# A four-layer graph network on one core: layer 0 begins with x in chunks, and layers 2 and 3 become one run of steps

## The chip, the core and the metric

The kernel runs on one core of a Trainium2 chip. The core has five instruction streams that run side by side and wait for each other by semaphores: PE (TensorE: matrix products, into PSUM), DVE (VectorE), ACT (ScalarE: exp, tanh, square root, copies), POOL (GpSimd) and SP (SyncE, which here only issues DMAs). DMAs issued by SP go through one queue and those issued by POOL through another; both are carried by the core's 16 DMA engines. The metric is device time in microseconds (us); lower is better. PE has a granted clock, which the profile shows as a share of full speed.

## The reference

The input is x, 2708 nodes by 512 features, and adj, a dense 0/1 matrix of 2708 x 2708 with 1.2% ones and a full diagonal. Four layers follow each other, each as x = layernorm(x + layer(x)):

- **Layer 0**, four heads of 128 features. Per head: Xw = X W, f1 = Xw v1, f2 = Xw v2, and an attention softmax over the neighbours of sigmoid(f1[i] + f2[j]). It is applied to Xw, then batch norm, a dense block with elu, batch norm, the same attention again on the result, the product with W transposed, elu, and a second dense block.
- **Layer 1**: adj times (x W + b), divided by the column sums of adj.
- **Layer 2**: h = x edge_w; scores h h^T, masked by adj, softmax along a row; adj times a softmax over nodes times that, applied to x weight.
- **Layer 3**: full attention: query, key and value projections, scores scaled, plus adj twice, softmax, applied to the values.

The first part of layer 0 and layers 2 and 3, as the reference has them:

```python
Xw = jnp.einsum('hnd,hde->hne', Xh, W)
f1 = jnp.einsum('hnd,hd->hn', Xw, V[:, 0, :, 0])
f2 = jnp.einsum('hnd,hd->hn', Xw, V[:, 1, :, 0])
sig = jax.nn.sigmoid(f1[:, :, None] + f2[:, None, :])
...
h = x @ edge_w
e = jnp.where(adj > 0, h @ h.T, NEG_BIG)
edge_att = jax.nn.softmax(e, axis=1)
output = adj * (node_att * edge_att) @ (x @ weight) + bias
...
a = (x @ Wq + bq) @ (x @ Wk + bk).T * scale + adj_matrix + spatial_matrix
attn = jax.nn.softmax(a, axis=-1) @ (x @ Wv + bv)
```

## The kernel before

All of it is float32. The nodes are cut into NT = 22 blocks, 21 of 128 and a last one of 20.

**Who sets the order.** The kernel is written in program order, but a planner in the language lays the instructions out: from its own estimate of times it puts on each engine the instruction that comes first in program order among those that are ready, and it gives out tile buffers ("bufs" of a tag in a pool) as they come free. On the chip each engine then works through its list in that order and waits where it has to. So an instruction can move ahead of others when its inputs and a buffer are free, and SP's list of DMA issues is in that order too.

**Start of layer 0** (`project`, L199). SP loads the parameters (L77), w0T (L190), w0, v1, v2 (L205 to L208) and then xT in four loads, each of 128 feature rows by all 2708 nodes (L210). PE makes w v1 and w v2 (L213). f1 is needed in two shapes. For the first pair of heads and the first half of the nodes it is made directly on all 128 partitions (`f1b`): matmuls with w v1 repeated 128 times as the stationary operand (L223), copied out by DVE and ACT (L227). For the rest it is made as rows (L231: 32 columns per head, six chunks of nodes), copied (L239), stored in DRAM as f1_d by POOL (L240), and loaded back by SP, spread over the partitions (L363). Then the values: for each of the 22 blocks, four heads of X W together with f2 go to a PSUM tile pxw (L245), which ACT or DVE copies to xw (L253), and DVE takes f2h out (L257). pxw lives under the PSUM tags po0 to po2.

**Attention of layer 0** (`attention_pass`, L285, called with first=True for the first attention, and again for the second). The loops run over two halves of the destination nodes (hf), two pairs of heads (p), and the 22 source blocks (jt). One step of it (`form`, L309): SP loads a block `a` of adjT, 128 x 1354 (L315, four buffers); in the first pair of each half DVE turns it into a mask (L330, L331) and POOL stores that as adj_d (L335); ACT takes tanh of f1b plus f2h for two heads (L341); DVE adds a constant and multiplies by the mask (L349); ACT takes exp (L350). PE then multiplies with the values: 2 heads x 3 column chunks into six accumulators `po`, tags po0 to po2 again (L397), and sums with ones (L420). The tiles po are allocated ahead of the loops (L354). The broadcast f1b of each later pair has two buffers and is loaded at L363 as early as a buffer allows.

**Layers 2 and 3** (`softmax_layer`, L1024, called once for each). The 22 blocks of destination nodes form 7 groups: six of three blocks, and the last of four (blocks 18 to 21). For each group there are 22 score steps and 22 sum steps, one per source block. A score step (`one_score`) loads a block of adjT columns (a_cols), makes scores by PE (L1106, `ps_s`), masks or biases them on DVE (L1397 or L1454) and keeps a running maximum (L1154). In layer 2 the scores are symmetric, so blocks already computed are stored, loaded again as s_kept, and transposed (L1098). At the end of a group `spread_max` brings the maximum of each row to all partitions, by transposes (L1166) and a product with ones (L1177). A sum step (`one_sum`) subtracts the maximum on DVE (L1197), takes exp on ACT (L1198), adds to the row sums (L1208), in layer 2 multiplies by adj (L1400), and PE multiplies with the values into `po` (L1213). The values are `sup` in layer 2 and the x rows themselves, `xs`, in layer 3, where the projection by wv comes after (`project`, L1288). At a group's end `end` takes reciprocals and queues the rest in `later`: in layer 2 the residual (L1406), the layer norm, and the transposes into hT, the keys and queries of layer 3 (L1412).

The steps of all groups are one sequence of 154. The sum step of number t - 25 is traced with the score step of number t:

```python
lag = NT + AHEAD
for t in range(steps + lag):
    if t < steps:
        ... one_score(states[gi], k)
    if t >= lag:
        ... one_sum(states[gi], k)
```

So the last 25 steps of a layer have sums and no scores. The two layers open their buffers (`att`, `att_ps`) each for itself; layer 3 begins when layer 2 has ended and its buffers and `sup` are given back. It then loads mqk (the product of wq and wk transposed, L1435), wv (L87) and bv (L92), and projects its first query (L1015).

Of the kernel before, what the change touches and what calls it, by code (L numbers as in the profile page):

```python
# [17 lines left out]
P = 128  # L18
# [11 lines left out]
def gnn_stack_kernel(  # L30
# [46 lines left out]
    nc.sync.dma_start(prm_sb, prm)  # L77
# [78 lines left out]
    with ExitStack() as l0:  # L156
# [31 lines left out]
        nc.vector.tensor_scalar(bm1, prm_sb[:, MB_DEC, :], 1.0, None, ALU.subtract)  # L188
        w0T_sb = p0.tile([P, H, P], F32, name="w0T_sb")
        nc.sync.dma_start(w0T_sb, w0T)  # L190
# [8 lines left out]
        def project(att, psum):  # L199
# [5 lines left out]
            nc.sync.dma_start(w0x[:, :, :P], w0)  # L205
            v12 = att.tile([P, H, 2], F32, tag="v12", name="v12", bufs=1)
            nc.sync.dma_start(v12[:, :, 0], v1)
            nc.sync.dma_start(v12[:, :, 1], v2.rearrange("(h e) -> e h", h=H))  # L208
            for c in range(C):
                nc.sync.dma_start(xT_sb[:, c, :], xT[c * P : (c + 1) * P, :])  # L210
# [6 lines left out]
            wv1 = held[:, H * (P + 2) : H * (2 * P + 2)].rearrange("p (h e) -> p h e", h=H)  # L217
            nc.vector.tensor_copy(wv1, w0x[:, :, P : P + 1].to_broadcast([P, H, P]))
            f1b = att.tile([P, HP, HW], F32, tag="f1b", name="f1b")
            for k in range(HP):  # L220
                for q, (q0, w) in enumerate(HCH[0]):
                    pf = psum.tile([P, HP, BANK], F32, tag=f"po{q}", name="pf")[:, k, :]
                    nc.tensor.matmul(  # L223
                        pf[:, :w], wv1[:, k, :], xT_sb[:, k, q0 : q0 + w], start=True, stop=True
                    )
                    copy = nc.scalar.copy if q % 2 else nc.vector.tensor_copy
                    copy(f1b[:, k, q0 : q0 + w], pf[:, :w])  # L227
            for ci, (c0, w) in enumerate(CHUNKS):
                pf = psum.tile([P, BANK], F32, tag=f"psm{ci % 2}", name="pf")
                for h in range(H):  # L230
                    nc.tensor.matmul(  # L231
                        pf[32 * h : 32 * h + 32, :w],
                        wv1[:, h, :32],
                        xT_sb[:, h, c0 : c0 + w],
                        start=True,
                        stop=True,
                    )
                f1c = att.tile([P, BW], F32, tag="rs", name="f1c")
                nc.vector.tensor_copy(f1c[:, :w], pf[:, :w])  # L239
                nc.gpsimd.dma_start(f1_d[:, c0 : c0 + w], f1c[0 : 32 * H : 32, :w])  # L240
            for jt, (j0, n) in enumerate(BLOCKS):
# [10 lines left out]
                copy = nc.vector.tensor_copy if jt % 3 == 2 else nc.scalar.copy  # L252
# [11 lines left out]
            copies(xw[:, NT - 1, :])  # L264
            copies(f2h[:, NT - 1, :])
            return f1b
# [18 lines left out]
        def attention_pass(values, first, att, psum, finish, f1b=None):  # L285
# [23 lines left out]
            def form(hf, p, jt, att, prepare, f1b, tv):  # L309
# [3 lines left out]
                a = att.tile([P, HW], F32, tag="a", name="a", bufs=4 if first else 3)  # L313
                src = adjT if prepare else adj_d
                nc.sync.dma_start(a[:n, :w], src[j0 : j0 + n, h0 : h0 + w])  # L315
# [33 lines left out]
                nc.vector.scalar_tensor_tensor(tv, tv, GUARD, ab, ALU.add, ALU.mult)  # L349
                nc.scalar.activation(tv, tv, AF.Exp, scale=0.5)  # L350

            later = []

            both = [  # L354
                psum.tile([P, HP, BANK], F32, tag=f"po{q}", name="po", bufs=1) for q in range(HB)
            ]
            po = [both[q][:, k, :] for k in range(HP) for q in range(HB)]
            for hf, (h0, w) in enumerate(HSPAN):
                for p in range(H // HP):
                    prepare = first and p == 0  # L360
                    if f1b is None or not prepare or hf > 0:
                        f1b = att.tile([P, HP, HW], F32, tag="f1b", name="f1b", bufs=2)
                        nc.sync.dma_start(  # L363
                            f1b[:, :, :w],
# [1173 lines left out]
```

## Time and profile before

| what | us |
|---|---|
| median of 3 runs | 3347.64 (3344.58 to 3348.74) |
| the profiled execution | 3344.3 |
| its span, first to last instruction | 3342.5 |
| PE busy | 3251.5 |
| first attention product of layer 0 begins | 52.71 |
| layer 2 begins (first score) | 1686.16 |
| layer 3 begins (first score) | 2389.58 |

A line of the profile's timeline gives start and length in us, engine, line of the kernel, operation, output<-inputs, shape, and how many such instructions it merges; in brackets the idle time of the engine just before it and what ended it. A line of the waits gives engine, tile and line of who waited, "<-" whom it waited for, then total us, how many times, and the longest. A line of the stretches gives the window, its length, the busy us of PE, PE's weight loads, DVE, ACT and POOL with counts, then PE's granted clock, the busy share of the DMA engines and GB/s. PE's ends are modelled, so a busy PE is not always at its peak.

### The profile page before, as it was taken

How to read it: one execution, taken by the hardware profiler on the slowest of the kernel's cores; microseconds unless marked ns; L12 is line 12 of the kernel's file. 1: busy time of each engine (PE TensorE's matmuls, PEld its weight loads, DVE VectorE, ACT ScalarE, POOL GpSimd, SP SyncE). 2: the span in 40 equal slices, each digit the busy share in tenths (PEclk: the TensorE clock that was granted, in tenths of full speed). 3: DMA queues.
4: the chain of work that ended last, by engine and by line, in shares of the span. 5: the costliest groups of instructions: out<-in, count | busy, mean ns of one | idle time of the engine just before them, and what ended most of it. 6: DMA issues, size and time to landing. Idle time of an engine off the chain costs nothing.

```text
span 3342.5 us, 30573 instructions
## 1 busy us (share of the span) xinstructions
PE 3251.5 (97%) x10980; PEld 1741.6 (52%) x10980; DVE 1988.9 (60%) x3227; ACT 1347.6 (40%) x1518; POOL 130.7 (4%) x212
## 2 busy tenths in 40 slices
PE   8999999999999989999999999999999999999998
PEld 5444444544444445885555555444455555555554
DVE  7868978767687585445135677776253443443533
ACT  6888887468877652001133333332011010110110
POOL 1100100000000000000010000000000000000001
PEclk9999999999999999999999999999999999999999
DMA  7655753335535412540044444553211111111100
GB/s 284 248 172 187 275 195 102 121 106 185 187 126 166 152 40 76 144 129 15 0 129 127 122 129 131 148 146 95 70 44 36 42 33 42 40 34 45 33 23 20
DMA packets 168576, 367.58 MB, mean 110 GB/s; under 512 B 20870, under 2 KB 111710, under 8 KB 165032
## 3 DMA queue, kind: packets, MB, share of 16 engines
q1 hardware_dynamic: 153448, 301.77, 30.2%
q0 software_dynamic: 14976, 63.86, 5.1%
q8 instruction: 86, 1.41, 0.2%
q14 instruction: 66, 0.54, 0.0%
HBM read 301.67 MB, written 63.35 MB: 109 GB/s over the span
## 4 chain that ended last, share of the span: by engine, by line
PE 72%; issue 13%; DVE 9%; DMA 3%; ACT 3%; POOL 1%; SPq 0%; POOLq 0%; DVEq 0%; ACTq 0%
PE po L1213 21%; PE ps_s L1106 17%; PE po L397 9%; PE ps_nb L954 6%; PE ps_wide L1015 4%; DVE t L349 3%; PE ps_hid L118 2%; PE ps_sup L1356 2%; PE ps_o L1291 2%; PE ps_mlp L637 1%; DMA a<-adj_d 1%; PE ps_dec L733 1%; ACT t L341 1%; DMA a_cols<-in_adjT_dram 1%; ACT t L350 1%
## 5 line engine op out<-in xcount | busy, mean ns | idle before, releaser
L349 DVE SCALAR_TENSOR_TENSOR t<-t,a 128x2708 f32<-128x2708 f32 (+1 forms) x162 | 480.0, 2975 | 142.4 <-ACT t L341 140.4
L341 ACT ACTIVATE t<-f1b,f2h 128x1354 f32<-128x1354 f32 (+1 forms) x324 | 445.8, 1414 | 87.9 <-PE psm L420 42.7
L350 ACT ACTIVATE t<-t 128x2708 f32<-128x2708 f32 (+1 forms) x162 | 396.7, 2452 | 71.1 <-DVE t L349 69.7
L397 PE MATMUL po<-t,xw 128*128 128x452 f32 (+3 forms) x1056 | 416.2, 557 | 8.1 <-ACT t L350 4.0
L397 PE MATMUL po<-t,emb 128*128 128x452 f32 (+3 forms) x1056 | 404.4, 552 | 16.7 <-ACT t L350 9.0
L1213 PE MATMUL po<-sup,e 128*128 128x512 f32 x882 | 410.3, 602 | 5.5 <-DVE e L1400 5.3
L1213 PE MATMUL po<-e,xs 128*128 128x384 f32 (+1 forms) x1176 | 407.5, 489 | 0.0
L1106 PE MATMUL ps_s<-q,hT 128*128 128x384 f32 (+1 forms) x1176 | 403.5, 489 | 0.0
L1454 DVE SCALAR_TENSOR_TENSOR e<-a_cols,ps_s 128x384 f32<-128x384 f32 (+1 forms) x154 | 85.6, 556 | 419.3 <-PE ps_s L1106 396.2
L397 PEld LDWEIGHTS po<-t,emb 128*128 128x128 f32 (+1 forms) x1056 | 195.6, 192 | 218.9 <-issue 195.0
L1106 PEld LDWEIGHTS ps_s<-q,hT 128*128 128x128 f32 x1176 | 222.6, 190 | 161.5 <-issue 6.5
L397 PEld LDWEIGHTS po<-t,xw 128*128 128x128 f32 (+1 forms) x1056 | 190.8, 192 | 220.6 <-issue 201.8
L1213 PEld LDWEIGHTS po<-e,xs 128*128 128x128 f32 x1176 | 221.6, 190 | 157.2 <-issue 6.0
L1213 PEld LDWEIGHTS po<-sup,e 128*128 128x128 f32 x882 | 161.6, 192 | 176.4 <-issue 149.6
L98 ACT ACTIVATE ln_rstd<-ln_rstd 128x1 f32<-128x1 f32 x88 | 17.2, 201 | 494.1 <-DVE ln_rstd L97 493.5
L1106 PE MATMUL ps_s<-hT 128*128 128x384 f32 (+5 forms) x672 | 212.3, 461 | 2.4 <-DVE e L1397 1.7
L1396 ACT ACTIVATE a_cols<-a_cols,neg_big 128x384 f32<-128x384 f32 (+1 forms) x154 | 94.8, 617 | 239.1 <-DMA a_cols<-in_adjT_dram 202.2
L954 PE MATMUL ps_nb<-hid_hi,at 128*128 128x512 f32 x484 | 185.6, 390 | 1.1 <-DVE at L947 1.1
L954 PE MATMUL ps_nb<-hid_lo,at 128*128 128x512 f32 x462 | 179.9, 389 | 0.0
L1190 ACT COPY nmax<-pb 128x384 f32<-128x384 f32 (+1 forms) x14 | 6.7, 480 | 424.9 <-PE pb L1177 345.6
L1208 DVE TENSOR_TENSOR acc<-acc,e 128x384 f32<-128x384 f32 (+2 forms) x294 | 162.5, 553 | 12.2 <-ACT e L1198 2.3
L1106 PEld LDWEIGHTS ps_s<-hT 128*128 128x128 f32 x672 | 122.4, 190 | 88.3 <-issue 17.8
(237 smaller groups left out, 3494.4 us busy)
## 6 DMA issues: line engine op xcount, KB each, us to landing
a<-adj_d SPq DMA_DIRECT2D x116, 677.0 KB
a_cols<-in_adjT_dram SPq DMA_DIRECT2D x378, 192.0 KB
a<-in_adjT_dram SPq DMA_DIRECT2D x42, 677.0 KB
adj_d<-a POOLq DMA_DIRECT2D x42, 677.0 KB, 4.6
raw<-in_adjT_dram SPq DMA_DIRECT2D x105, 256.0 KB
kept<-t POOLq DMA_DIRECT2D x10, 1354.0 KB, 6.5
t<-kept SPq DMA_DIRECT2D x10, 1354.0 KB
a_cols<-in_adjT_dram SPq DMA_DIRECT2D x63, 202.0 KB
```

The costliest lines, as they stand in the source:

```text
L118: nc.tensor.matmul(ps[:n], xt[:, c, :n], w[:, c, :], start=(c == 0), stop=(c == C - 1))
L341: nc.scalar.activation(tv[:, k, :], f1b[:n, k, :w], AF.Tanh, bias=f2h[:n, jt, h : h + 1], scale=0.5,)
L349: nc.vector.scalar_tensor_tensor(tv, tv, GUARD, ab, ALU.add, ALU.mult)
L350: nc.scalar.activation(tv, tv, AF.Exp, scale=0.5)
L397: nc.tensor.matmul(po[HB * k + q][:, :qw], values[r : r + n, jt, h * P : (h + 1) * P], t[r : r + n, k, q0 : q0 + qw], start=(jt == 0), sto ...
L954: nc.tensor.matmul(pos[it], at, half[:, jt, :], start=(jt == 0 and k == 0), stop=(jt == NT - 1),)
L1015: nc.tensor.matmul(ps[:, :width], w(c, o), xt(c), start=(c == 0), stop=(c == C - 1),)
L1106: nc.tensor.matmul(ps[:, b * P : w], keys[:, c, j0 : j0 + P], st["q"][:, c, b * P :], start=(c == 0), stop=(c == C - 1),)
L1208: nc.vector.tensor_tensor(acc, acc, e[:m], ALU.add)
L1213: nc.tensor.matmul(out, lhsT, rhs, start=(k == 0), stop=(k == NT - 1))
L1396: nc.scalar.activation(a, a, AF.Identity, bias=neg_big[: a.shape[0]], scale=1.0e30)
L1454: nc.vector.scalar_tensor_tensor(e, a, 2.0, ps, ALU.mult, ALU.add)
```

## The change

**Layer 0, start.** The loads of xT are now six chunks of 450 or 452 nodes, each with all 512 features, in the order: v2, v1, w0T, chunk 0, w0, chunks 1 to 3, the first block of adjT, chunk 4, the second block, chunk 5, the parameters. f1b is no longer made by 128-wide matmuls. f1 is made as rows for the first three chunks (the first half of the nodes, all heads), collected in one tile, stored to f1_d by SP, and loaded back by SP, spread over the partitions. The third and fourth block of adjT are issued after that spread. The values are traced for 17 blocks; the other five, the f1 rows of the second half, the copies of the last block and bm1 are traced by `rest` after the first `form`, and those of them that run on DVE are ordered behind its L349. Up to block 13 ACT copies the values, from block 14 on DVE. The tiles po are allocated after that.

**Later f1b.** The load of f1b for each later pair is ordered behind the ninth-last load of `a` traced so far in the same pass.

**Layers 2 and 3.** `softmax_layer` opens no buffers of its own and no loop; it returns a score step and a sum step, and one loop runs those of both layers. Layer 3's score steps begin 12 steps after layer 2's last one, thus beside layer 2's last 13 sum steps; its sums follow 25 steps later. Layer 3's group 0 takes the source blocks in order 0 to 21, and its block 18 comes after the norms of blocks 18 to 21. mqk is loaded into buffers of s_kept and s_raw. What else layer 3 needs lies in the blocks of `sup` that layer 2 has finished with (`room`): the queries in blocks 0 to 7, wv in 8 to 11, bv in 12, oT in 13 to 16, and four output tiles y (two before) in 17 to 20. The tile quarters moves from the constants to the pool of the keys, so it is computed after layer 1. The output rows of the last group are stored by SP instead of POOL.

The core of the diff, without what is only indented anew:

```diff
+            nc.sync.dma_start(v12[:, :, 1], v2.rearrange("(h e) -> e h", h=H))
             nc.sync.dma_start(v12[:, :, 0], v1)
-            for c in range(C):
-                nc.sync.dma_start(xT_sb[:, c, :], xT[c * P : (c + 1) * P, :])
+            nc.sync.dma_start(w0T_sb, w0T)
+            blocks = []
+            for ci, (c0, w) in enumerate(CHUNKS):
+                nc.sync.dma_start(
+                    xT_sb[:, :, c0 : c0 + w],
+                    xT[:, c0 : c0 + w].rearrange("(c p) j -> p c j", p=P),
+                )
+                if ci == 0:
+                    nc.sync.dma_start(w0x[:, :, :P], w0)
+                if HB <= ci and len(blocks) < 2:
+                    j0 = P * len(blocks)
+                    a = att.tile([P, HW], F32, tag="a", name="a", bufs=4)
+                    nc.sync.dma_start(a[:, : HSPAN[0][1]], adjT[j0 : j0 + P, : HSPAN[0][1]])
+                    blocks.append(a)
+            nc.sync.dma_start(prm_sb, prm)
...
-            for k in range(HP):
-                for q, (q0, w) in enumerate(HCH[0]):
-                    pf = psum.tile([P, HP, BANK], F32, tag=f"po{q}", name="pf")[:, k, :]
-                    nc.tensor.matmul(
-                        pf[:, :w], wv1[:, k, :], xT_sb[:, k, q0 : q0 + w], start=True, stop=True
-                    )
-                    copy = nc.scalar.copy if q % 2 else nc.vector.tensor_copy
-                    copy(f1b[:, k, q0 : q0 + w], pf[:, :w])
...
+            h0, w = HSPAN[0]
+            for ci, (q0, _) in enumerate(HCH[0]):
+                f1_rows(ci, stage[:, q0:])
+            nc.sync.dma_start(f1_d[:, h0 : h0 + w], stage[0 : 32 * H : 32, :w])
+            spread = nc.sync.dma_start(
+                f1b[:, :, :w], f1_d[:HP, h0 : h0 + w].partition_broadcast(P)
+            )
...
+            AT_ONCE = NT - 5
+            for jt in range(AT_ONCE):
+                values_of(jt)
+            def rest(step):
+                with tc.issue_after(step.ins):
+                    for jt in range(AT_ONCE, NT):
+                        values_of(jt)
+                    for ci in range(HB, NCH):
+                        c0, w = CHUNKS[ci]
+                        f1c = att.tile([P, BW], F32, tag="rs", name="f1c")
+                        f1_rows(ci, f1c)
+                        nc.gpsimd.dma_start(f1_d[:, c0 : c0 + w], f1c[0 : 32 * H : 32, :w])
+                    copies(xw[:, NT - 1, :])
+                    copies(f2h[:, NT - 1, :])
...
+                    early = prepare and hf == 0 and jt < len(blocks) + 2
+                    with tc.issue_after(spread.ins) if early else nullcontext():
+                        loads.append(
+                            nc.sync.dma_start(a[:n, :w], src[j0 : j0 + n, h0 : h0 + w])
+                        )
...
+                        with tc.issue_after(loads[-9].ins) if len(loads) > 8 else nullcontext():
+                            nc.sync.dma_start(
+                                f1b[:, :, :w],
+                                f1_d[HP * p : HP * (p + 1), h0 : h0 + w].partition_broadcast(P),
+                            )
...
-    quarters = const.tile([P, C, Q], F32, name="quarters")
+    quarters = featp.tile([P, C, Q], F32, name="quarters")
...
+                return late if gi else list(range(NT))
...
+        def room(first, blocks, *shape):
+            t = sup[:, first : first + blocks, :].rearrange("p t f -> p (t f)")
+            ...
+            q = room(4 * (gi % 2), 4, C, GW)
...
+            y = room(17 + it % 4, 1, F)
...
+                queue = nc.sync if it in GROUPS[-1] else nc.gpsimd
+                queue.dma_start(out[i0 : i0 + n, :], y[:n])
...
+        steps = len(GROUPS) * NT
+        lag = NT + AHEAD
+        start3 = steps + 12
+        assert start3 + GROUPS[-1][0] >= steps + lag + GB
+        for t in range(start3 + steps + lag):
+            if t == steps:
+                weights3()
+            if t == steps + lag:
+                values3()
+            if t < steps:
+                score2(t)
+            elif 0 <= t - start3 < steps:
+                score3(t - start3)
+            k = None
+            for first, step in ((lag, sum2), (start3 + lag, sum3)):
+                if 0 <= t - first < steps:
+                    step(t - first)
+                    k = (t - first) % NT
+            if later and (k is None or (k % 2 and k < NT - 1)):
+                later.pop(0)()
```

## The prediction

> **What bounds the kernel now.** I read the totals first, then the waits of PE by stage, then the timeline at the three places that the change touches, and the stretches for clock and DMA. Totals of the page, busy time per engine:
>
> ```profile
> PE 3251.5 (97%) x10980; PEld 1741.6 (52%) x10980; DVE 1988.9 (60%) x3227; ACT 1347.6 (40%) x1518; POOL 130.7 (4%) x212
> ```
>
> PE is idle for 91 us of 3342.5. No matmul of layers 1 to 3 is removed, so the change can only win idle PE time, slow-clock time, and prologue work. The start, in the timeline (start, length, what):
>
> ```profile
> 10.59 5.76 PE L223 MATMUL pf<-xT_sb,held 128*128 128x452 f32 x8 [2.09 <-DMA xT_sb<-in_xT_dram]
> 27.66 2.75 ACT L341 ACTIVATE t<-f1b,f2h 128x1354 f32<-128x1354 f32 x2
> 32.80 2.97 DVE L349 SCALAR_TENSOR_TENSOR t<-t,a 128x2708 f32<-128x2708 f32 x1
> 36.17 2.48 ACT L350 ACTIVATE t<-t 128x2708 f32<-128x2708 f32 x1
> 52.71 13.91 PE L397 MATMUL po<-t,xw 128*128 128x452 f32 x36
> ```
>
> PE starts when the first row block of xT has landed (10.46), but the first attention product starts at 52.71: its PSUM tiles are those of the value projection (pxw, L242), whose 22 blocks leave PSUM by ACT and DVE between the tanh, exp and mask steps of the first tiles. From there each step is 4.75 us of products and 1.28 us of sums (chain: L397 x12, L420 x16), 6.03 us, and PE is full until 160 us. The junction of layers 2 and 3:
>
> ```profile
> 2366.34 1.02 PE L1279 MATMUL ps_po<-po,quarters 128*20 128x512 f32 x2
> 2373.57 3.45 PE L1005 MATMUL tp<-ident,xs 128*128 128x128 f32 x16 [6.21 <-DVE xs L113]
> 2377.33 12.41 PE L1015 MATMUL ps_wide<-hT,mqk 128*128 128x384 f32 x32 [0.32 <-ACT hT L1008]
> 2389.58 2.74 PE L1106 MATMUL ps_s<-q,hT 128*128 128x384 f32 x8
> ```
>
> PE has nothing to do while DVE normalises the last four blocks. The waits of PE over layers 2 and 3 (total, times, longest):
>
> ```profile
> PE tp L1005 <- DVE xs L113: 7.3, 3, 6.2
> PE po L1213 <- DVE e L1400: 5.3, 4, 3.9
> ...
> PE ps_wide L1015 <- ACT hT L1008: 0.3, 1, 0.3
> ```
>
> The 6.2 us are the junction. The 3.9 us (at 2293) begin the last group's sums, when scores have run out.
>
> **Start of layer 0.** Removed: 12 matmuls that made f1b on PE (L223, 5.76 + 1.71 us by the chain) and their six copies; bm1, quarters and the parameters leave the head of DVE's and SP's order. Added: a store of f1 (four rows of 1354) and a broadcast load of 1354 KB, both on SP. Moved: x comes in six chunks of 904 KB instead of four rows of 1354 KB; only 17 of 22 value blocks precede the first mask step, and ACT evacuates 14 of them undisturbed.
>
> When does the spread land? SP's order becomes two v's, w0T (256 KB), chunk 0, w0 (256), chunks 1, 2, 3, a0 (677), chunk 4, a1 (677), chunk 5. Rates, from the stretches (the last three fields are PE's granted clock, DMA share and GB/s):
>
> ```profile
> 12.00:14.00 2.00, 2.00 (x4) 0.94 (x3) 0.63 (x1) 0.02 (x1) 0.00 (x0) 1.00 1.02 433
> 1162.00:1164.00 2.00, 2.00 (x7) 0.98 (x6) 1.96 (x4) 0.00 (x0) 0.00 (x0) 1.00 1.05 383
> 28.00:30.00 2.00, 2.00 (x20) 1.31 (x12) 1.97 (x4) 2.00 (x2) 0.00 (x0) 1.00 0.05 12
> ```
>
> Rows of xT ran at 433; chunks of the new shape are already loaded at L836, at 383: 2.35 us each. Today 1.89 MB are ahead of the first use, 4.4 us at 433, and land at 10.46, so 6.1 us is start and latency. After: 0.6 + 2.35 + 6.1, less 0.2 of issue, gives chunk 0 at **8.9**; then chunk 1 (with w0) 11.8, chunk 2 14.2, chunk 3 16.6, a0 18.1, chunk 4 20.5, a1 22.0, chunk 5 **24.4**. f1 of chunk 2 takes 0.86 (L231 x16, 1.72 for two chunks) and a copy of 0.62: the store is issued at about 16. The row nearest to it, f_d<-f1c, lands in 2.3 us (median), which would be 18.3. But those stores went by Pool's queue. [...] then the store, though issued at 16, waits behind chunk 3 to chunk 5, all issued by 8. The trace's own landing order fits that (xT at 10.46 and on to 20.4, then the four a until 26). [...] store landed at 25, not 18.3. The spread then takes what f1b took at 584.60 (ACT's wait on it ended at 590.94): 6.3 us, so f1b at **31.4** (by the 2.3 us row: 24.8). Behind the waiting store on SP stand the spread, a2 and a3; a2 lands near 33 and is needed only at 46.
>
> Then tanh twice 2.8 (34.2), mask step 2.97 (37.2), exp 2.45 (39.7). PE meanwhile: 3 x 0.86 of f1 and 17 blocks at 0.98 (L245, 24 matmuls in 2.95), some 2.5 us of slow clock, from 8.9: 31, so all ready. After the mask step DVE owes five blocks at 0.83 (xw 0.68, f2h 0.15) and three f1 copies at 0.62: 6.0 us, the last block's copies at 41.4. Products start at **41.5**, not 52.7. But today sums of two steps (2.6 us) are done by then, and steps 1 to 3 are in hand. After, step 1's mask comes at 43.3 + 2.97, exp at 48.8, step 2 (DVE: 0.86 + 1.57 + 2.97 = 5.4 a step) at 54.2. PE ends step 2 at 54.8 + 6.0 = 60.8, against 67.91 today: **-7.1**. DVE's 5.4 stays under PE's 6.03, so it holds. Ends: -11 (store lands at once) and +3 (the spread 10 us later, each microsecond then costing one).
>
> f1b of later pairs is held behind the ninth-last load. In the first pass it lands eight steps early, hidden by 48 us. In the second pass it moves from 590 to about 745, where loads of a are on the chain (3.85 us each); SP issues it while the next load waits for a buffer 5 us, longer than its 4.2 us of transfer at 329 GB/s (585 to 591). **0**; uncovered +4.
>
> **Junction.** From the end of L1279 (2367.36) to the first score (2389.58) are 22.2 us. The work in it at full clock: 16 transposes 1.82 (row at 1658.78) and the projection 10.32 (row at 2570.07). Layer 3's scores, 2.58 us each, are traced beside and behind the last sums; twelve of them (31 us) follow the sums while the four norms (6.2 us to the first transpose) go on. So 22.2 - 12.1 = **-10.1**. Of it 6.5 is idle, 3.7 is slow clock:
>
> ```profile
> 2373.00:2380.00 7.00, 6.12 (x20) 4.29 (x21) 2.06 (x6) 2.04 (x5) 3.70 (x5) 0.50 0.61 211
> 2446.00:2452.00 6.00, 3.20 (x7) 1.60 (x7) 2.85 (x8) 0.33 (x1) 0.00 (x0) 0.78 0.14 41
> ```
>
> [...] where the rows show 1.6 + 2.1. I take the rows[...]. [...] That stall (2.8 idle at the first maximum, 3.1 slow) stays: when layer 3's group 1 begins, no sums run yet. The 3.9 us at 2293 stay too: layer 3 begins nine steps later, and its q lies in value blocks 0 to 3 that those sums still read. Ends: -16 (projection fills 2293, with its slow clock), 0 (see rivals). mqk (4 x 256 KB) is queued on SP before the last sums' columns and waits for s_kept, last used at 2280; DMA is nearly empty there (33 GB/s), five column buffers cover it: 0, at worst +3. Layer 3 otherwise keeps PE at 100% (2460 to 3310): 0.
>
> **quarters** moves from DVE's idle prologue (9.08 to 10.64) to where layer 1's memory comes free. hT's memset, from the same memory, ran at 1526.58, just ahead of the copies that PE waits for (0.59 us, xt_g): **+1.6**; ends 0, and +4 if the clock drops.
>
> **End.** The last rows wait 1.15 us for Pool (y, L1459); four y buffers save 0.65, SP's issue (0.33 against Pool's 0.52 and its 0.3 of start) some 0.35: **-1.0**, ends -1.5 and 0.
>
> **Sum:** -7.1 - 10.1 + 1.6 - 1.0 = -16.6. The profiled execution took 3344.3 (span 3342.5); it becomes 3327.7. The median before is 3.3 above it, so **3331.0**. About 0.2% (6.7 us) is what a measurement can tell here.
>
> **Rivals.** (1) *The start gains nothing.* The store waits longer, or the planner lets step 1 starve: f1b at 38.5 or later. For it: a write and a dependent read in series on a loaded queue. Against: after 26 us the DMA stands idle (12 GB/s). 3331.0 + 7.1 = 3338.1. (2) *The junction gains nothing:* the planner leaves layer 3's first scores behind the norms, or the wait reappears at group 1. Against: elsewhere in layers 2 and 3 transposes after a norm cost PE only 1.1 us (7.3 - 6.2). 3331.0 + 10.1 = 3341.1, just no change. (3) *Slower:* q, y, oT, wv and bv now all lie in sup; if accesses are ordered by the whole tile, every oT copy, y and q waits for a score in flight, say three waits of 2.6 us a group: 7 x 7.8 = 55, **3386**. It decides from 3.3 us a group (16.6 + 6.7 over 7). Against it: hT is written block by block while scores read it, and PE waited 0.3 us for that in all.
>
> **From cases to numbers.** The forecast 0.66, rival 1 0.16, rival 2 0.10, rival 3 0.08. The forecast's own range is 3321 to 3338 (start -11 to -2, junction -14 to -8, quarters up to +3). The range 3318 to 3343 takes in rivals 1 and 2. Faster: 0.65 + 0.12 + 0.04 = 0.81; same 0.01 + 0.03 + 0.06 = 0.10; slower the rest, 0.09.
>
> **What would show it.** Start: the spread's issue near 25, first tanh near 31, first product near 41, L397's third step ended near 61. Junction: no PE wait of L1005 over 1 us, and projection rows of 10.3 us for group 0; layer 3's scores between sums of layer 2. quarters beside hT's memset, with a PE wait near 2 us. The forecast is wrong if the first tanh comes after 38, if PE waits on sup's writers in layer 3, or if a new wait of several us stands at the end of layer 2.

## The result

The changed kernel takes 3331.64 us (median of 5 runs, 3330.47 to 3335.33). The kernel before, run beside it, takes 3346.38 (3343.53 to 3348.74). The ratio is 0.9958, with a 95% interval of 0.9944 to 0.9973: faster by 0.4%. A second series of the same two kernels gave 3331.66 and 3349.17, ratio 0.9945 (0.9933 to 0.9957). The profiled span went from 3342.5 to 3328.7, that is by -13.8.

The totals of the changed kernel's page:

```profile
span 3328.7 us, 30525 instructions
PE 3238.2 (97%) x10968; PEld 1735.7 (52%) x10968; DVE 1986.9 (60%) x3224; ACT 1346.3 (40%) x1515; POOL 126.1 (4%) x205
```

PE is busy for 13.3 us less. 7.5 of these are the 12 matmuls of f1b that are gone (5.76 + 1.71 in the prediction's rows); the rest fits the mean granted clock, 0.987 before and 0.989 after. Idle PE time is 90.5 us where it was 91.0: new waits have taken the place of those that went.

The start, in the timeline (start, length, what), from two answers, of all engines and of PE alone:

```profile
18.59 0.62 SPq L250 DMA_DIRECT2D f_d<-f_rows  x1
24.61 0.37 SPq L251 DMA_DIRECT2D f1b<-f_d  x1
32.59 6.68 ACT L380 ACTIVATE t<-f1b,f2h 128x1354 f32<-128x1354 f32 x5 [4.33 <-DMA f1b<-f_d]
35.59 2.97 DVE L388 SCALAR_TENSOR_TENSOR t<-t,a 128x2708 f32<-128x2708 f32 x1
```

```profile
16.90 0.96 PE L238 MATMUL pf<-xT_sb,held 128*32 128x450 f32 x8
17.79 6.09 PE L259 MATMUL pxw<-held,xT_sb 128*128 128x130 f32 x52
...
39.38 3.71 PE L259 MATMUL pxw<-held,xT_sb 128*128 128x130 f32 x15 [4.39 <-DVE f2h L272]
...
43.10 1.25 PE L238 MATMUL pf<-xT_sb,held 128*32 128x450 f32 x5
44.27 4.05 PE L450 MATMUL po<-t,xw 128*128 128x452 f32 x10
```

The fourth step's products, where the third step is over, before and after:

```profile
67.84 4.82 PE L397 MATMUL po<-t,xw 128*128 128x452 f32 x12
```

```profile
62.36 4.82 PE L450 MATMUL po<-t,xw 128*128 128x452 f32 x12
```

The first attention product starts at 44.27 (52.71 before), and the third step is over at 62.36 (67.84 before): -5.48. The f1 rows of chunk 2 wait in PE's order behind value blocks until 16.90, and those of the last chunk stand right ahead of the first product. From 39.38 to there PE doesn't wait; its granted clock is 0.50 from 39.4 to 42.5.

The junction of layers 2 and 3, in PE's timeline:

```profile
2328.14 10.48 PE L1068 MATMUL ps_wide<-hT,mqk 128*128 128x384 f32 x32
2338.46 2.74 PE L1166 MATMUL ps_s<-sup,hT 128*128 128x384 f32 x8
2341.04 2.74 PE L1273 MATMUL po<-sup,e 128*128 128x512 f32 x6
```

```profile
2411.87 1.03 PE L1339 MATMUL ps_po<-po,quarters 128*20 128x512 f32 x2
2412.83 8.01 PE L1166 MATMUL ps_s<-sup,hT 128*128 128x384 f32 x24
2420.68 0.60 PE L1058 MATMUL tp<-ident,xs 128*128 128x128 f32 x4
...
2438.57 0.30 PE L1226 MATMUL tp_mx<-ident,mx 128*128 128x128 f32 x1 [1.32 <-DVE mx L1214]
...
2442.65 12.51 PE L1068 MATMUL ps_wide<-hT,mqk 128*128 128x384 f32 x32
```

The first query is projected among layer 2's sums and at full clock (10.48 for 32 matmuls; 1.00 from 2328 to 2340), scores and sums alternate, and after the last matmul of the sums (L1339) three scores of 2.7 us cover the first norm. The transposes at 2420.68 carry no wait. The stall at group 1's maximum has stayed, and the projection behind it again takes 12.51 instead of 10.48 (granted clock 0.50 from 2440 to 2443).

The waits of PE over layers 2 and 3 (total, times, longest):

```profile
PE po L1273 <- DVE e L1463: 4.8, 3, 3.9
...
PE tp L1058 <- DVE xs L112: 1.1, 2, 0.6
...
PE ps_s L1166 <- ACT sup L1417: 0.7, 1, 0.7
```

The wait on xs is down from 7.3 (longest 6.2) to 1.1 (longest 0.6).

Where the 13.8 us lie, by the time of the same matmul in both timelines:

| stretch | place, before and after | predicted | measured |
|---|---|---|---|
| start of layer 0 | third step over, 67.84 and 62.36 | -7.1 | -5.5 |
| later f1b, first pass | to the product at 279.64 and 278.31 | 0 | +4.2 |
| rest of layers 0 and 1 | to 1525.40 and 1522.33 | 0 | -1.7 |
| quarters | to layer 2's first score, 1686.16 and 1685.09 | +1.6 | +2.0 |
| inside layer 2 | to the wait at 2297.19 and 2297.87 | 0 | +1.8 |
| junction | to group 1's projection, 2451.42 and 2442.65 | -10.1 | -9.45 |
| inside layer 3 | to 3318.12 and 3309.04 | 0 | -0.3 |
| end | to the end of the span | -1.0 | -4.7 |
| sum | | -16.6 | -13.8 |

### The profile page after: what moved, and what is told of

The parts are those of the page before. It is cut to its first block, busy times and chain, and to the rows that moved or that the text cites. A ratio compares the mean times of both kernels' runs of the same rounds, so it can differ in the third digit from the quotient of the medians.

```text
span 3328.7 us, 30525 instructions
## 1 busy us (share of the span) xinstructions
PE 3238.2 (97%) x10968; PEld 1735.7 (52%) x10968; DVE 1986.9 (60%) x3224; ACT 1346.3 (40%) x1515; POOL 126.1 (4%) x205
## 4 chain that ended last, share of the span: by engine, by line
PE 78%; issue 11%; DVE 6%; ACT 2%; DMA 2%; POOL 1%; SPq 0%; POOLq 0%; DVEq 0%; ACTq 0%
PE po L1273 23%; PE ps_s L1166 17%; PE po L450 11%; PE ps_nb L1007 6%; PE ps_wide L1068 4%; PE ps_hid L117 2%; PE ps_sup L1410 2%; PE ps_o L1351 2%; PE ps_dec L786 2%; DVE t L388 2%; PE ps_mlp L690 1%; ACT t L380 1%; ACT t L389 1%; PE psm L473 1%; DMA a<-adj_d 1%
## 5 line engine op out<-in xcount | busy, mean ns | idle before, releaser
L388 DVE SCALAR_TENSOR_TENSOR t<-t,a 128x2708 f32<-128x2708 f32 (+1 forms) x162 | 480.2, 2975 | 149.2 <-ACT t L380 145.6
L1166 PE MATMUL ps_s<-sup,hT 128*128 128x384 f32 (+1 forms) x1176 | 406.8, 490 | 0.0
L1166 PEld LDWEIGHTS ps_s<-sup,hT 128*128 128x128 f32 x1176 | 221.9, 190 | 164.2 <-issue 14.4
```

The source lines that it names most:

```text
L388: step = nc.vector.scalar_tensor_tensor(tv, tv, GUARD, ab, ALU.add, ALU.mult)
L1166: nc.tensor.matmul(ps[:, b * P : w], keys[:, c, j0 : j0 + P], st["q"][:, c, b * P :], start=(c == 0), stop=(c == C - 1),)
```

## The experiments

Each alteration is made to the changed kernel. Line numbers in an experiment's rows are its own; they differ by a few from those of the changed kernel.

| run | median, us | span of its profile | ratio to the kernel before (95%) |
|---|---|---|---|
| after_again | 3331.66 | 3326.2 | 0.9945 (0.9933 to 0.9957) |
| noedge | 3333.51 | 3332.5 | 0.9952 (0.9940 to 0.9963) |
| quart | 3325.93 | 3325.1 | 0.9933 (0.9921 to 0.9945) |
| quart_again | 3327.73 | 3329.0 | 0.9934 (0.9920 to 0.9947) |
| best1 | 3330.07 | 3328.3 | 0.9944 (0.9931 to 0.9957) |
| pooltail | 3334.29 | 3331.8 | 0.9958 (0.9946 to 0.9970) |
| storepool | 3332.79 | 3333.5 | 0.9951 (0.9938 to 0.9965) |
| late3 | 3336.41 | 3332.8 | 0.9967 (0.9956 to 0.9979) |
| adj3 | 3330.47 | 3330.2 | 0.9948 (0.9936 to 0.9960) |
| alate | 3334.23 | 3327.1 | 0.9959 (0.9946 to 0.9971) |
| a1late | 3327.84 | 3329.8 | 0.9941 (0.9929 to 0.9954) |
| best2 | 3323.56 | 3321.8 | 0.9926 (0.9914 to 0.9939) |

The runs of one kernel lie up to 15 us apart (late3, 3329 to 3345), so the verdicts below come from the traces, from the place that an alteration touches; medians are read with the scatter in mind.

**The unaltered kernel again.**

> The kernel after the change, unaltered, for its scatter and as the base of the other runs of this call. Expected: median 3331 to 3333, the profile's waits where they were (3.4 us at 243.7, 2.6 us at 1526, 3.9 us at 2297), and stretches of slow clock in other places of layers 0 and 1 and as many as before, each worth about 1.7 us.

It came out as expected. The waits were 3.14 (at 244.15), 2.58 (at 1524.23) and 3.93 (at 2295.90), and the span was 2.5 us shorter than the first profile's, without any alteration.

**The hold on f1b taken away** (noedge).

```diff
-with tc.issue_after(loads[-9].ins) if len(loads) > 8 else nullcontext():
+with nullcontext():
```

> The broadcast loads of f1b for the later pairs go back to the place in the order that they had before the change (issued as soon as the planner gives them out, not behind the ninth-last load of a); everything else as after the change. Theory: the f1b load, 1354 KB, issued at 225.09 on the load queue directly ahead of a load of a, delays the mask of a step near 240 and gives the 3.38 us wait of PE at 243.70; without the hold the wait is again under 1 us, the gain at that place stays near -5.5 us instead of -1.3, and the kernel takes 3331.6 - 3 to 4.4 = 3327 to 3329. Rival: the wait comes from the order of DVE's and ACT's work around the pair's change, not from the load: the wait of about 3 us at 243 stays and the time is 3331 to 3332.

The orders of PE, ACT and POOL are those of the changed kernel; SP's order differs, and two DVE instructions stand elsewhere in the second pass. The stall is gone. ACT and PE of the changed kernel around it, then PE without the hold:

```profile
231.51 2.46 ACT L389 ACTIVATE t<-t 128x2708 f32<-128x2708 f32 x1 [0.42 <-DVE t L388]
237.25 4.05 ACT L380 ACTIVATE t<-f1b,f2h 128x1354 f32<-128x1354 f32 x3 [3.28 <-DVE t L388]
```

```profile
243.70 6.51 PE L450 MATMUL po<-t,xw 128*128 128x452 f32 x12 [3.38 <-ACT t L389]
```

```profile
241.37 4.82 PE L450 MATMUL po<-t,xw 128*128 128x452 f32 x12 [0.59 <-ACT t L389]
```

So the load of f1b causes the wait, but not in the way that I had written down. ACT waits for a free buffer t. One of these buffers is being stored by POOL to kept (1354 KB), for the second pass. The row of that store, first of the changed kernel, then without the hold (start of its issue, then the time from issue to landing):

```profile
L432 POOL DMA_DIRECT2D kept<-t x1: 547/547/547, 227.4 to 227.4; - x1
...
DMA to landing us min/median/max: 9.7/9.7/9.7
```

```profile
L432 POOL DMA_DIRECT2D kept<-t x1: 549/549/549, 227.9 to 227.9; - x1
...
DMA to landing us min/median/max: 5.0/5.0/5.0
```

227.44 + 9.7 = 237.14, and ACT goes on at 237.25. The row puts this wait down to DVE's L388, which happens to end at that moment; the run without the hold shows that the tanh doesn't need it, for there it starts at 234.91 while L388 runs. The f1b load, issued at 225.09, is under way together with the store of 227.44 (the DMA engines are 0.96 busy from 227.4 to 237.1), and the store takes 4.7 us longer. All fourteen profiles agree: where such a load is issued 2.3 us ahead of the store, the store takes 9.1 to 9.7 us (eleven profiles), and without it 5.0 to 5.1 (three).

The time was not better, though. The gain at the product after the stall was 3.9 us (274.37 against 278.31), and 2.3 were left at 444 and none at 582. Slow clock took it back, a part of it between 300 and 320. The 32 products of one column (L524) there, without the hold and then in the kernel quart, which has it:

```profile
302.35 6.99 PE L524 MATMUL po<-prm_sb,enc_w 128*128 128x1 f32 x32
```

```profile
302.59 3.87 PE L524 MATMUL po<-prm_sb,enc_w 128*128 128x1 f32 x32
```

From 298 to 320 the granted clock is 0.69 in the one and 0.92 in the other. The slow clock comes in whole pieces: stretches cut at the right places show 0.50 for a full 3.41 us, or for several of these in a row. First the changed kernel, then quart:

```profile
303.16:306.57 3.41, 2.63 (x28) 1.77 (x29) 3.41 (x5) 3.41 (x5) 0.00 (x0) 1.00 0.28 113
306.57:309.98 3.41, 3.41 (x18) 3.41 (x18) 0.94 (x2) 3.41 (x4) 0.55 (x1) 0.50 0.52 202
...
316.81:320.22 3.41, 3.41 (x22) 1.29 (x21) 3.41 (x3) 0.88 (x2) 0.56 (x1) 1.00 0.86 340
```

```profile
302.63:306.04 3.41, 3.41 (x35) 3.41 (x31) 2.24 (x3) 3.41 (x4) 0.55 (x1) 1.00 0.27 102
306.04:309.45 3.41, 3.41 (x7) 1.77 (x7) 2.95 (x4) 2.06 (x2) 1.15 (x2) 0.50 0.28 110
309.45:312.87 3.42, 3.42 (x13) 1.49 (x15) 3.38 (x4) 2.46 (x1) 0.00 (x0) 1.00 0.46 111
```

Here the changed kernel has three slow pieces, quart one, and noedge four (300.16 to 313.81). A piece in which PE works all the time loses half of it, 1.7 us (the 12 products at 243.70, with the piece of 245.13 in them, take 6.51 for 4.82). Within one profile all slow pieces lie on one grid: in the changed kernel they begin at 245.13, 306.57, 446.52 and 600.12, the last three 18, 59 and 104 times 3.413 us behind the first. From profile to profile the grid lies elsewhere against the program (by 0.23 to 0.96 of a piece at the place below).

The number of slow pieces goes with this place. Just ahead of these 32 products PE waits 1.2 us for DVE (t, L467). Over the fourteen profiles, three slow pieces come where that wait ends at 0.23 to 0.40 of a piece behind the grid's last mark, one at 0.47 to 0.66, two at 0.71, and four at 0.79 to 0.96. The three kernels without the hold (noedge, best1 and the one before) lie at 0.79 to 0.96 and show 6.99 for the 32 products; the eleven others show 3.7 to 6.3. So the longer slow stretch goes with the place on the grid, and it is not shown that the hold has any part in it.

**quarters among the constants** (quart, and once more as quart_again).

```diff
-quarters = featp.tile([P, C, Q], F32, name="quarters")
+quarters = const.tile([P, C, Q], F32, name="quarters")
```

> The quarters tile lies among the constants again and is written in DVE's prologue, not where layer 1's memory comes free. Theory: PE's wait of 2.58 us at 1526.44 on xt_g falls back to 0.6 and the first score of layer 2 comes 2.0 us earlier; the time is 3331.6 - 2.0 = 3329.6. Rival: the two microseconds are taken up again by the small waits inside layer 2, which DVE sets (about 1.8 us were lost there after the change): 3331 to 3332 although the wait is gone. A second rival: the prologue copies delay the first tanh or mask at the start by as much (0.5 to 1.5 us).

> The same kernel as in the run with the quarters tile among the constants, on the same chip as the three other runs of this call. The first time its median was 5.7 us under the kernel after the change, of which the trace shows 2.0 us as the removed wait. Theory: 2.0 us is the gain and the rest scatter of the slow-clock stretches in layers 0 and 1: 3328 to 3330. Rival: all of it belongs to the alteration: 3326.

PE's wait at the start of layer 2, changed kernel and quart:

```profile
1526.44 1.98 PE L1410 MATMUL ps_sup<-w_sb,xt_g 128*128 128x512 f32 x4 [2.58 <-DVE xt_g L1061]
```

```profile
1524.42 2.84 PE L1410 MATMUL ps_sup<-w_sb,xt_g 128*128 128x512 f32 x6 [0.58 <-DVE xt_g L1061]
```

2.0 us are won, at the place expected, and the start of layer 0 doesn't suffer (first tanh at 32.80 against 32.59). Among the last norms of layer 1 and the copies that PE waits for, DVE makes quarters in the changed kernel (1523.48 to 1526.58). The medians are 5.7 and 3.9 us under the changed kernel's, the trace accounts for 2.0; the rest fits the scatter, but it was not shown to be that. Two profiles of this one kernel differ by 3.9 us in their spans, and the granted clock differs in the same direction: 21 slow pieces in one and 25 in the other (the end of the span left out), three of the four more in layer 0 between 550 and 1000.

**Both together** (best1).

> Two alterations together: the quarters tile among the constants, and the broadcast loads of f1b not held back behind a's loads. Theory: the two gains add (each removes a wait of PE of its own: 2.0 and 3.9 us); 3326 - 3.9 = 3322. Rival: what is won at 243 is lost again by slow clock in the second half of layer 0 (as in the run without the hold, where the time of 446 to 910 us grew by 5 us): 3325 to 3327, no gain over quarters alone.

Neither number came: 3330.07 lies above even the rival's 3325 to 3327. In kind the rival was right, for nothing was gained over quart (3325.93 and 3327.73). Both waits are gone (no wait over 0.6 at 243, 0.58 at 1527), but the same work from 275 to 445 takes 169.8 us, where it takes 164.9 in quart and 168.2 in the changed kernel; after 300 there are four slow pieces, as in noedge. So taking the hold away removes a stall, and in two kernels it won no time; as a net cost my 0 isn't contradicted. Whether the medians' missing gain is the clock's alone is open.

**The last stores on Pool's queue** (pooltail).

```diff
-queue = nc.sync if it in GROUPS[-1] else nc.gpsimd
+queue = nc.gpsimd
```

> The last group's rows are stored by Pool's queue again; the four y buffers stay. Theory: the end of the program waits about 4 us longer behind a store issued by Pool than behind one issued by SP, so from the last DVE instruction to the end of the span it takes 6.7 us again and not 2.6, and the time is 3331.6 + 4 = 3335.6. Rival (my prediction's sizes): the issue alone is worth 0.35 us, the rest of the shorter end comes from the buffers of y: 3332.0, and the end after the last DVE instruction is about 3 us.

The last DVE instruction, and in the second the store behind it, first of the changed kernel and then of pooltail:

```profile
3325.53 0.53 DVE L112 TENSOR_SCALAR sup<-sup,ln_mv,ln_rstd 20x512 f32<-20x512 f32 x1
```

```profile
3324.56 0.53 DVE L112 TENSOR_SCALAR sup<-sup,ln_mv,ln_rstd 20x512 f32<-20x512 f32 x1
3325.38 0.52 POOL L1555 DMA_DIRECT2D out_dram<-sup  x1 [2.90 <-DVE sup L112]
```

From DVE's end to the end of the span it is 3328.7 - 3326.06 = 2.64 with SP, and 3331.8 - 3325.09 = 6.71 with POOL (6.73 in the kernel before). The theory holds: 4.07 us go with the queue, and the four buffers of y have little part in it. The four last stores of pooltail land 1.8 to 2.3 us after their issue, the last one at 3327.2, so the span runs on for 4.6 us after it.

**f1's store on Pool's queue** (storepool), **and less data under way** (alate, a1late). What makes the store land 6.0 us after its issue?

```diff
-nc.sync.dma_start(f1_d[:, h0 : h0 + w], stage[0 : 32 * H : 32, :w])
+nc.gpsimd.dma_start(f1_d[:, h0 : h0 + w], stage[0 : 32 * H : 32, :w])
```

> The store of f1's first half goes by Pool's queue and not by SP's; the spread that reads it stays on SP. Theory [...]: on SP's queue the store waits behind the x chunks and a's issued before it; on Pool's queue it lands some 2.3 us after its issue, the spread is issued near 21.5 and not 24.6, and the first tanh comes near 29.5 and not 32.6; the start gains 3 us, the first product comes near 42 and not 44.3 (limited by the copies of the value blocks), and the time is about 3329.5. Rival: the store was late because SP was blocked in its own issues and because the DMA engines are shared by all queues; on Pool's queue it lands as late, the first tanh stays within 1 us of 32.6, and the time is 3331 to 3332. A third possibility: the spread now competes with the chunks that are still under way and delays a chunk; then the first tanh is earlier, but the first product isn't.

```diff
-                if HB <= ci and len(blocks) < 2:
...
+            while len(blocks) < 2:
+                j0 = P * len(blocks)
+                a = att.tile([P, HW], F32, tag="a", name="a", bufs=4)
+                with tc.issue_after(spread.ins):
+                    nc.sync.dma_start(a[:, : HSPAN[0][1]], adjT[j0 : j0 + P, : HSPAN[0][1]])
+                blocks.append(a)
```

(In a1late the first line stays, with 1 in place of 2.)

> The first two loads of a (677 KB each) are issued behind the spread and no longer between the x chunks; the rest as after the change. The question is what makes the store of f1 land 6.0 us after its issue (18.59 to 24.61) where stores on Pool's queue take 2.3 us as a median. Theory: the store waits until the data that other loads have under way on the same DMA engines has landed, 1354 KB of it a; without a the x chunks are in by about 21, the store lands 3 us earlier (spread issued near 21.5), the first tanh comes near 29, and then the first mask waits for a0 (behind the spread, near 31.5, and 2.4 us of DVE): mask near 34 and not 35.6, first product near 43, time 3331.7 - 1 = 3330.5. Rival: the store takes its 6 us whatever else is under way (its own price of small rows and a write): spread issued near 24.5, a0 only near 34, mask at 36.5, first product 1 us later than 44.3, time 3332.5.

> Only the second load of a goes behind the spread. Theory (shared engines): the store lands some 1.7 us earlier (677 KB at about 390 GB/s less ahead of it), spread issued near 22.9, first tanh near 31, mask near 34 with a0 ready in time, first product near 42.7 (limited by the copies that DVE owes behind the mask), time 3330. Rival: as above, the store's 6 us don't change; first tanh near 32.6, time 3331 to 3332, and the second step may wait for a1.

The store and the spread that waits for it, in storepool, then alate, then a1late:

```profile
19.47 0.79 POOL L250 DMA_DIRECT2D f_d<-f_rows  x1 [17.95 <-DVE f_rows L245]
25.13 0.37 SPq L251 DMA_DIRECT2D f1b<-f_d  x1
```

```profile
19.00 0.62 SPq L245 DMA_DIRECT2D f_d<-f_rows  x1
21.25 0.38 SPq L246 DMA_DIRECT2D f1b<-f_d  x1
...
27.84 8.00 ACT L381 ACTIVATE t<-f1b,f2h 128x1354 f32<-128x1354 f32 x6 [0.24 <-DVE f2h L273]
```

```profile
19.11 0.63 SPq L250 DMA_DIRECT2D f_d<-f_rows  x1
22.70 0.38 SPq L251 DMA_DIRECT2D f1b<-f_d  x1
```

On the other queue the store takes 5.7 us, much like the 6.0 on SP's: the rival held, with the first tanh at 33.30. Without the two blocks of a ahead of it, it takes 2.25, without one 3.6. So in these four runs the store waits for what other loads have under way, whichever queue issues it. The end fits a sum to within 0.8 us: w0T, w0, six chunks and two a are 7.46 MB, at 392 GB/s (12 to 16 us) 19.0 us, and with 6.1 of start and latency 25.1; measured 24.61. For alate 6.07 MB at 383 give 22.0; measured 21.25.

The prediction's 25 had the store wait on SP's queue behind the chunks issued ahead of it. For the number that was enough, but the queue of issue isn't what matters here (5.7 us on POOL's, 6.0 on SP's). By what means loads under way hold the store up was not shown.

What came of the earlier spread: in alate the first tanh is at 27.84 and the first product at 40.86, 3.4 us earlier, but the second step then waits 2.67 us for its mask (at 49.97): its a is issued later, so DVE works on it only behind the first mask step, and in between waits 1.06 us for a store of f1 rows to land. The third step is over at 62.02 (62.36 in the changed kernel). In a1late the first product is at 42.05 and the third step is over at 60.84, 1.5 us earlier. In both, the wait at 243 is gone as well: the store of kept still takes 9.2 and 9.3 us behind a load of f1b, but it is issued some 4 us sooner (223.9 and 223.26) and has landed before ACT needs the buffer. Here the order of the instructions changed too, so this second effect can't be put down to one cause. As medians, alate shows no gain (3334.23), and a1late is 3.8 under the changed kernel.

**Layer 3 started later** (late3 behind all norms, adj3 right behind the last sum).

```diff
-        start3 = steps + 12
+        start3 = steps + lag + 6
```

(In adj3: `steps + lag`.)

> Layer 3 starts at step lag + 6 after layer 2's scores and not at step 12: its first query and scores come behind all sums and all norms of layer 2; the one set of buffers and the one run of steps stay. Theory: the gain of the junction is the scores that fill the time of the last four norms; without them PE waits about 6 us on xs again and runs some 3.5 us of the projection at half clock, so the second group's projection comes 9 to 10 us later and the time is 3331.6 + 9.5 = 3341. Rival: the old junction's wait came from the change of buffers and pools between the layers (a barrier), which is gone here too; then PE waits 1 to 2 us only and the time is 3332 to 3334.

> Layer 3 starts at the step behind the last sum of layer 2 (step lag): no score of it lies between the sums, but its projection is in PE's order ahead of the last norms' transposes or between them. Theory: what counts is work that needs no norm of the last blocks; the projection of the first query (10.5 us) and the scores behind it fill the time of the norms just as well as scores among the sums do, so PE's wait on xs is under 1.5 us and the time is 3331 to 3333. Rival: scores must be among the sums, since the sums of the last group else wait for DVE and the norms come due with nothing in hand: 2 to 5 us lost, 3334 to 3337.

The junction in late3, then in adj3:

```profile
2370.17 3.45 PE L1058 MATMUL tp<-ident,xs 128*128 128x128 f32 x16 [6.29 <-DVE xs L112]
2373.75 12.60 PE L1068 MATMUL ps_wide<-hT,mqk 128*128 128x384 f32 x32
...
2448.02 11.23 PE L1068 MATMUL ps_wide<-hT,mqk 128*128 128x384 f32 x32
```

```profile
2370.99 10.59 PE L1068 MATMUL ps_wide<-hT,mqk 128*128 128x384 f32 x32 [1.84 <-DVE rs L1333]
2381.41 2.74 PE L1166 MATMUL ps_s<-sup,hT 128*128 128x384 f32 x8
2383.99 0.60 PE L1058 MATMUL tp<-ident,xs 128*128 128x128 f32 x4
...
2444.73 11.93 PE L1068 MATMUL ps_wide<-hT,mqk 128*128 128x384 f32 x32
```

From the 3.93 us wait near 2295 to group 1's projection it takes 154.2 us in the kernel before, 154.6 in late3, 144.8 in the changed kernel and 145.7 in adj3. So the change of buffers and pools cost nothing by itself: late3 has none, and has the whole old stall, even to the 6.29 us and the slow clock behind it (3.45 us for 16 transposes, 12.60 for the projection). And scores among the sums aren't needed: adj3 has none before 2381, wins 8.9 of the 9.8 us, and PE finds the first norm done when the projection and one score are over. What counts is some 10 us of work that doesn't need the last norms. The median of late3, 3336.41, shows only half of the 9.5 expected; its seven runs are the most scattered here.

**The best of these together** (best2: quarters among the constants, the second block of a behind the spread).

> Two alterations together: the second load of a behind the spread, and the quarters tile among the constants. If both hold (2.0 us by quarters, 1.6 us by the start): 3331.7 - 3.6 = 3328. If the start's gain is lost in the places of slow clock: 3329 to 3331, like quarters alone.

3323.56 (3319.69 to 3325.61), ratio 0.9926: below both numbers expected, the fastest, and 8 us below the changed kernel's medians. The span is 4.4 and 6.9 below its two profiles. The trace shows 2.0 at quarters, and 4.3 to 5.5 at the last step of the first half (298.45 against 302.71 and 303.94), for the most part the wait at 243 that is gone. It is faster than both kernels, before and after.

## Why the prediction was right

3331.0 was predicted and 3331.64 measured. The junction's mechanism was right. The start's chain (loads, store, spread, mask, products) was right in its order and wrong in two of its links. Some sizes were off, in both directions, and the profile shows -13.8 for the sum of -16.6.

- **What bounds the kernel.** Right. What was won is prologue work, idle PE time and slow clock.
- **Start, -7.1; measured -5.5.** The store's landing came as predicted (24.6 for 25), but not for the reason given: the order on one queue doesn't decide it (5.7 us on POOL's queue, 6.0 on SP's), the bytes under way do (2.25 with 1354 KB less). The sum behind the 25 also counts the profile's KB, which are 1024 bytes, as 1000; this makes the chunks land some 0.4 us too early. The term "the spread takes 6.3" was mis-sized: it took 8.0. The loads of a behind it are not the reason, for in a1late three stand right behind it and it took 6.9, and in alate four and it took at most 6.6. What differs is POOL's store of the first mask (adj_d, 677 KB): in the changed kernel it is under way when the spread begins (23.81 to 28.31), in the two others it is issued behind the spread. No run isolates it, so this cause is open. The first mask was therefore late by 1.4 us (35.6 for 34.2). The term "products start when the last block's copies are done, 41.5" named the wrong wait: these copies run from 45.66 to 46.40, and the first product is ahead of them. PE waits 4.39 us until DVE, past the first mask step, has freed a pxw; then it has two value blocks and a chunk of f1 rows in its order ahead of the first product, and runs them without a further wait at half clock (0.50 from 39.4 to 42.5), so 44.27. Of these 2.8 us the prediction had already allowed 1.2 as a wait at the second step, which didn't come; -5.5 is left.
- **Later f1b, 0.** The step that failed is "it lands eight steps early, hidden by 48 us". The load was hidden. What was not seen is whom it collides with: the store of kept, 2.3 us behind it, whose buffer ACT needs again. This cost 4.2 us, the size of my "uncovered +4", but in the first pass and not in the second: 2.8 us of wait (3.38 for 0.59), and a slow piece behind it (6.51 for 4.82 at 243.70) that the second profile of the same kernel doesn't have. In the whole time the hold is no loss, as far as two kernels without it show; the slow clock in which the gain went is not shown to be the hold's.
- **Junction, -10.1; measured -9.45**, with its own place and cause, shown by late3. The slow clock was taken from the old stall's rows (1.6 + 2.1), and the term fits to 0.7 us. At the stall that stays no wait passes 1.32 us, and the projection takes 12.51 for 10.48.
- **quarters, +1.6; measured +2.0.** The wait went from 0.59 to 2.58, and the clock didn't drop behind it (1.00 from 1526.4 to 1540).
- **End, -1.0; measured -4.7.** Right in direction, the term for SP's issue mis-sized by a factor of ten: 4.07 for 0.35.
- **Inside layer 2, 0; measured +1.8.** Among the other profiles this stretch varies by 1.9 us, so I take no cause for it.

The rivals: the start did gain, and the junction did; late3 shows what the second rival would have looked like. The third, order by the whole tile of sup, is refuted: it foresaw some 55 us of waits on writers of sup in layer 3, and PE's waits list none there. The one of 0.7 us is at layer 2's first score, and was there before.

The prediction's closeness owes something to luck: the end gave 3.7 us more than counted, which paid for most of the f1b wait; and the kernel before ran 1.3 us under the median that the prediction started from (3346.38 for 3347.64).

## What to carry to other kernels

A transfer that is hidden itself is not free: ask which other transfer is under way in those microseconds, and which buffer is held until that one lands (here a store took 9.7 us for 5.0, and PE waited 3.38 us for 0.59). When an engine waits for a chain of norms at the end of a layer, put any work of about that length between, here 10 us; it need not be interleaved with the work before. And look at which queue issues the very last store (here 4.07 us).

## What was not expected of the hardware

- A last store issued by POOL makes the program end 4.07 us later than one issued by SP, from the last DVE instruction to the end of the span (6.71 against 2.64), though its data land at most 2.3 us after the issue.
- The store of f1's first half, with loads under way on SP's queue, landed 5.7 us after its issue on POOL's queue and 6.0 on SP's own; with 1354 KB less under way, 2.25.
- The slow clock comes in pieces of 3.41 us at 0.50, one to four in a row, on a grid that lies elsewhere against the program in every profile. The same wait of 1.2 us ahead of the same products was followed by one to four of them, and the number went with its place on the grid. So gains are made up for or hidden: the same kernel's spans differ by 2.5 (the changed one) and 3.9 us (quart).
- In quart the clock dropped behind a piece without idle time: PE counts as busy for all of 302.63 to 306.04 (3.41 us), all of it in products of one column, and the next piece, 306.04 to 309.45, is at 0.50.
